# Reading M before chunk 4 in a compressed-interaction kernel: order of loads and sums at the start, and one product handed to GpSimd

## The chip, the cores and the metric

The kernel runs on one core of a Trainium2 chip. The metric is the device time of one execution in microseconds; lower is better. TensorE (PE) multiplies matrices, VectorE (DVE), ScalarE (ACT) and GpSimd (POOL) work element by element, SyncE (SP) issues most DMAs. Every engine works through its own queue in program order.

## The reference

The reference is a compressed interaction network of three layers on `x` of shape (1024, 64, 16): a batch of 1024, 64 fields, 16 embedding values.

```python
x0 = x; h = x; xs = []
for i in range(3):
    z = einsum('bfe,bge->bfge', x0, h).reshape(B, f0 * fh, E)
    y = einsum('oc,bce->boe', Ws[i], z) + bs[i][None, :, None]
    if i != 2:
        x_i, h = y[:, :64, :], y[:, 64:, :]
    else:
        x_i, h = y, y
    xs.append(x_i)
pooled = sum(concatenate(xs, axis=1), axis=2)      # (1024, 256)
return pooled @ fc_w.T + fc_b                       # (1024, 1)
```

All is float32. `W0` is (128, 64·64), `W1` and `W2` are (128, 64·64) too, since each hidden half has 64 rows.

## The kernel before, in words

Only a weighted sum of the last layer is wanted, so the kernel folds the final vector into the weights. From `W2` and `fc_w` it makes a 64 x 64 matrix (V2), and contracts the second half of `W1` with it to a 64 x 64 x 64 tensor M. What remains for every chunk of the batch are the pairwise products of the fields, x_f · x_g, contracted with two sets of 64 columns: one gives the hidden half h1, the other q, which is later multiplied with h1. M enters only through M[f,g] + M[g,f].

**Chunks and tiles.** The batch is cut into 32 chunks of 32 items (512 columns each: 32 x 16). The distinct field pairs of a chunk fill 16 tiles of 128 rows, in four groups j = 0 to 3 of four tiles each. One `product` (L248) multiplies `xa` (four shifted copies of x, 1 MB) by one quarter `xb[j]` (256 KB) into a block of 128 x 2048; 14 such blocks (`z`) are handed out in turn, first freed first used (`take`, `used`). VectorE's products read `xb[j]` from a PSUM copy (`xp`), which ScalarE makes (`second`, L566) in a bank of a two-bank rotation ("y"). GpSimd's products read `xb[j]` where it was loaded.

**The head.** Chunks 2, 3, 0, 1 come first, while weights are still made. M is computed, written to a DRAM scratch array `md`, extended to 96 x 96 rows, and read back into the block `ms` on a slant: rows (`read_rows`, two reads on each of two queues) and columns (`read_columns(j)`, one read for each half of the partitions, 64 KB each in rows of 64 floats). The diagonal goes to `va`. `q_weights(j)` (L511) adds rows and columns on VectorE into the q half of `w_all` for the tiles of group j. `last_q_weights` does that for j = 3, returns the block, and clears 32 rows of one tile. `head_q_tile` (L280) then contracts the kept products of chunks 0 and 1 with these q columns, group after group. `w_sums` makes sums and differences of weights for later (`ws`), mostly on GpSimd.

**Chunks 4 and 5** are plain: all 16 tiles are contracted with both sets of columns. Beside them run small jobs on sums of weights: `weigh` (GpSimd), `add_up` (VectorE, L553) and `place` (ScalarE, L558) make `v0`, `va` and `vb`. `x_v0x` (L303) multiplies x by V0 x, read from the banks `y`.

**Pairs.** Chunks 6 to 29 go in twelve pairs (a, b) through a scheme that saves products of matrices by working with sums and differences. For a pair, VectorE makes products X (a, j = 0, 1), B21 (a, j = 2, 3), B22 (b, j = 2, 3) and T3 (from the sum of two quarters of b, `w_both`), by `w_product` (L646). GpSimd makes six differences by `w_mix` (L661): T2 = T3 - X, T3 = B22 - T2 and T2 = T2 - B21, each for j = 0 and 1, the last two in place. TensorE (`mm`, L538) adds them into three banks, `alpha`, `beta` and `delta`. `snap_p1` and `snap_p7` (ScalarE, L669, L675) copy from alpha and delta at the middle of the pair.

**Order.** From the head's q tiles on, the program is a list of jobs with a slot number each, `at(when, fn, ...)`; the list is sorted by the number and issued in that order. So a slot is no time: it only says what stands before what in each engine's queue, and in which order blocks and banks are handed out. The pair with index n = 0 (chunks 6 and 7, k = 3) has a line of slots of its own, relative to T0 = 33; its `make_pair` takes ten slots for B22 j=2, w_both 0, T3 0, X 0, B22 j=3, w_both 1, T3 1, X 1, B21 j=2, B21 j=3, and six for the differences. The loads in lines 485 to 507 are written out by hand: their order is that of SyncE's queue.

Of the kernel before, what the change touches and what calls it, by code (L numbers as in the profile page):

```python
# [42 lines left out]
F = 64  # L43
# [25 lines left out]
def cin_kernel(ctx, tc, xra, xrb, wh, w0r, w1h, w2t, wx1, wx0, vec, out):  # L69
    nc = tc.nc  # L70
# [6 lines left out]
    halves = [slice(0, F), slice(F, 128)]  # L77

    def const_tile(name, shape):
        return const.tile(shape, F32, tag=name, name=name)  # L80
# [4 lines left out]
    def take(uses=1):  # L85
        n = vacant.pop(0)
        left[n] = uses
        return n
# [28 lines left out]
    for base in (0, 64, -64):  # L117
        nc.gpsimd.affine_select(
            out=shift, in_=shift, compare_op=ALU.not_equal, fill=1.0, base=base,
# [12 lines left out]
    va, vb, v0 = (const_tile(n, [128, F]) for n in ("va", "vb", "v0"))  # L132
# [8 lines left out]
    def load_xa(c, at=slice(0, NI)):  # L141
        if c not in xas or at.start == 0:
            xas[c] = xp.tile([128, NI, N], F32, tag="xa", name=f"xa_{c}")
        nc.sync.dma_start(
            out=xas[c][:, at, :],
            in_=bass.AP(
                tensor=xra.tensor, offset=c * XR * N + at.start * N,
                ap=[[N, 128], [1, (at.stop - at.start) * N]],
            ),
        )  # L150

    def quarter(c, j):
        xbs.setdefault(c, {})[j] = xp.tile([128, N], F32, tag="xb", name=f"xb_{c}_{j}", bufs=9)
        return xbs[c][j]

    def load_xb(c, *js):
        for j in js or range(NJ):
            nc.sync.dma_start(out=quarter(c, j), in_=xrb[c, :, j, :])
# [223 lines left out]
    for h in range(2):  # L382
        at = slice(32 * h, 32 * h + 32)
# [36 lines left out]
    row = EXT * F  # L420

    def m_ap(f1, f2, dims):
        return bass.AP(tensor=md.tensor, offset=md.offset + f1 * row + f2 * F, ap=dims)
# [3 lines left out]
    for half, queue in enumerate((nc.sync, nc.scalar)):  # L427
        queue.dma_start(
            out=m_ap(0, 32 * half, [[row, F], [1, 32 * F]]), in_=m_rows[halves[half]]
# [5 lines left out]
        out=m_ap(64, 68, [[row, 4], [4 * F, 7], [1, 4 * F]]),  # L435
        in_=m_rows[0:4, 4 * F :].rearrange("p (k c) -> p k c", c=4 * F),
# [26 lines left out]
    def skewed(f1, f2, dims):  # L463

        at = len(dims) - 2
        return m_ap(f1, f2, dims[:at] + [[row + F, F]] + dims[at:])
# [4 lines left out]
    def read_columns(j, queue, half):  # L471
        queue.dma_start(  # L472
            out=ms[halves[half], 1, j * NI : (j + 1) * NI],
            in_=skewed(0, 16 * half + 4 * (j + 1), [[row, NI], [1, F]]),
        )
# [20 lines left out]

    for half in range(2):
        read_columns(1, nc.sync, half)
    load_xa(4)
    load_xb(4, 3, 0)  # L500
    for half in range(2):
        read_columns(2, nc.sync, half)
    load_xb(4, 1)
    for half in range(2):
        read_columns(3, nc.sync, half)
    nc.sync.dma_start(out=va[halves[1]], in_=m_ap(0, 0, [[row + F, F], [1, F]]))
    load_xb(4, 2)

    def q_weights(j):
        at = slice(j * NI, (j + 1) * NI)  # L510
# [17 lines left out]
    def at(when, fn, *args, **flags):  # L528
        ops.append((when, len(ops), fn, args, flags))
# [111 lines left out]
    wh_all, wq_all = w_all[:, :, 0:64], w_all[:, :, 64:128]  # L641
    s1, s2, s3, s4, neg = (ws[:, n] for n in range(5))

    def w_product(p, c, j, name, uses):
        p.setdefault(name, {})[j % 2] = b = take(uses)
        nc.vector.tensor_tensor(  # L646
            blocks[b], xas[c], xbs[c][j].unsqueeze(1).to_broadcast([128, NI, N]), ALU.mult
        )

# [43 lines left out]
    def make_pair(t, p, when, mixed):  # L693
        a, b = p["a"], p["b"]
        for when, c, j, name, uses in (
            (when[0], b, 2, "B22", 5), (when[1], b, 0, None, 0), (when[2], b, 0, "T3", 9),
            (when[3], a, 0, "X", 5), (when[4], b, 3, "B22", 6), (when[5], b, 1, None, 0),
            (when[6], b, 1, "T3", 9), (when[7], a, 1, "X", 12 if p["k"] > 3 else 6), (when[8], a, 2, "B21", 5),
            (when[9], a, 3, "B21", 6),
        ):  # L700
            if name is None:
                at(t + when, w_both, p, j)
                continue
            if name != "T3":
                at(t + when - (3.3 if p["k"] > 4 and name == "B22" and j == 2 else 2.7), second, c, j)
            at(t + when, w_product, p, c, j, name, uses)
        for when, j, *names in zip(
            mixed, (0, 1, 0, 1, 0, 1), *zip(
                *(2 * (("T2", "T3", "X"),) + 2 * (("T3", "B22", "T2"),) + 2 * (("T2", "T2", "B21"),))
            )  # L710
        ):
            at(t + when, w_mix, p, j, *names)

    def first_fill(p):
        a = p["a"]
        return [
            (w_job, p, beta, wq_all, NI, "X"), (w_job, p, beta, wq_all, NT - NI, "B21"),
            (lambda: q_extra(a, va, p["beta"]),),
        ]

    def second_fill(p):
        return [
            (w_job, p, delta, wh_all, NI, "X"), (w_job, p, delta, wh_all, NT - NI, "B21"),
        ] + w_run(p, delta, neg, "T2")[7 - p["late"] :]

    def late_run(p):
        b = p["b"]
        return [
            (w_job, p, alpha, neg, NI, "T3"), (w_job, p, alpha, s4, NI, "B22"),
        ] + w_run(p, alpha, s4, "B22") + [(lambda: q_extra(b, vb, p["alpha"]),)]  # L730
# [8 lines left out]
    def window(t, p, fill, late, pad=[], order=GROUPS[4:] + GROUPS[:4]):  # L739
        zipped(  # L740
            t,
            w_run(p, alpha, wq_all, "X", True, order=order) + fill[0] + w_run(p, alpha, s2, "T2")
            + fill[1] + w_run(p, alpha, s1, "T3")
            + [(w_job, p, alpha, wh_all, NI, "T3"), (w_job, p, alpha, s1, NI, "B22")],
            w_run(p, delta, s3, "T3", True) + late
            + w_run(p, beta, wq_all, "B21", True, 2 * NI)
            + pad + w_run(p, delta, neg, "T2")[: 7 - p["late"]],
        )
        at(t + 30.2, squares, p)
        at(t + 6.8, snap_p1, p)  # L750
        at(t + 6.9, snap_p7, p)
        at(t + 6.8 + len(fill[0]) + 7, snap_u2, p)

    def end_pair(t, p, whens):
        hb_, qa, uub, ha, uua, xv, add = whens
        at(t + hb_, w_hb, p)
        at(t + qa, w_qa, p)
        at(t + uub, w_uu, p, alpha, "A", snaps[2])
        at(t + ha, w_ha, p)
        at(t + uua, w_uu, p, delta, "O", snaps[0])  # L760
        at(t + xv, x_v0x, p["k"])
        at(t + add, sums, p["k"])


    def load_pair(t, p, b0, a0, b1, a1):
        a, b = p["a"], p["b"]
        at(t + b0, load_xa, b)
        at(t + b0, load_xb, b, 2, 0)
        at(t + a0, load_xa, a)
        at(t + a0, load_xb, a, 0)  # L770
        at(t + b1, load_xb, b, 3, 1)
        at(t + a1, load_xb, a, 1, 2, 3)
        for c in (b, a):
            at(t + 1, load_e, c)
            at(t + 14, square, c)
        at(t + 1.1, load_xx, p["k"])
# [19 lines left out]
        at(-17, new_acc, c, tag="set")  # L796
    for m in range(NT):
        at(m - 16, head_q_tile, 0, m // NI, m % NI)
    at(-11, q_weights, 2)
    at(-7, last_q_weights)  # L800
    at(-16, w_sums, 0)
    at(-6.9, w_sums, 1)
    for j, when in enumerate((-12.3, -10.5, -6)):
# [39 lines left out]
    for n in range(NPAIR):  # L843
        k = n + 3
        s = k % 2
        p = {
            "k": k, "A": halves[s], "O": halves[1 - s], "b": 2 * k + s, "a": 2 * k + 1 - s,
            "late": 1 + n % 2 if n else 0,
        }
        pairs.append(p)  # L850
        t = T0 + SPAN * n
        if n == 0:
            load_pair(t, p, -39.9, -33.3, -33.15, -27)
            make_pair(
                t, p, (-23.4, -20.7, -20.4, -17.8, -17.2, -16.8, -16.6, -12.5, -4, 3),
                (-14, -12.4, 7.2, 12.4, 16.4, 21.7),
            )
            left5 = [[(contract_half, 5, 3, i, n) for i in (2, 3)] for n in range(2)]
            window(
                t, p, ([left5[1][0], (q_extra, 4, va)], [left5[1][1]]),  # L860
                [left5[0][0], (q_extra, 5, va), None, None], [left5[0][1], None],
                GROUPS,
            )
        else:
            q = pairs[-2]
            load_pair(t, p, -34, -28, -27.8, -27.7)
            make_pair(
                t, p, (-21.4, -18.7, -18.4, -15.8, -12.2, -9.5, -6.1, -2, 1.6, 4.2),
                (-5, 2.8, 7.2, 12.4, 16.4, 21.7),
            )  # L870
            window(t, p, (first_fill(q), second_fill(q)), late_run(q))
            end_pair(t, q, (0.7, 11.7, 17.9, 22.3, 23.2, 24, 27.5))
# [45 lines left out]
    c, k = NCH - 1, NP - 1  # L918
    t, q = T0 + SPAN * NPAIR, pairs[-1]
# [151 lines left out]
```

## Time and the profile before

| | |
|---|---|
| Time, median of 3 runs | 471.14 us (468.98 to 473.04) |
| Profiled execution | 469.04 us, span 467.2 us, mean clock 0.996 |
| TensorE busy | 457.5 us, 98% of the span |
| VectorE busy | 398.1 us, 85% |
| GpSimd busy | 329.9 us, 71% |
| ScalarE busy | 118.7 us, 25% |
| DMA | 86.04 MB, mean 184 GB/s |

A line of the profile's groups reads: line of the code, engine, operation, output<-input, times done, busy time. A wait reads "engine, line, output <- who ended it", then the total, the number and the longest. The slices divide the span into 40 parts of 11.7 us; a digit is a tenth. The span leaves out 1.8 us that the execution's own time has around it.

### The profile page before, as it was taken

To read this page: it belongs to the slowest core of one execution; us is meant where nothing else is said; L and a number is where in the kernel's file an instruction comes from. 1 tells how busy PE (TensorE), PEld (TensorE's weight loads), DVE (VectorE), ACT (ScalarE), POOL (GpSimd) and SP (SyncE) were. 2 spreads that over 40 slices of the span, in tenths; PEclk is the share of its full clock that TensorE was granted. 3 is DMA by queue.
4 is the path that set the end of the run, shared out by engine and by line. 5 is a ranking of instruction groups with operands and counts; after the bars stand their busy time and mean duration, and the time that the engine had idled before them with its cause. 6 is when DMAs were issued, how large, how long until landed. Compare 5 with 4: busy or idle time off the path is not lost.

```text
span 467.2 us, 6049 instructions
## 1 busy us (share of the span) xinstructions
PE 457.5 (98%) x2308; PEld 169.1 (36%) x2308; DVE 398.1 (85%) x283; ACT 118.7 (25%) x219; POOL 329.9 (71%) x99
## 2 busy tenths in 40 slices
PE   8999699998999999999999999999999999999997
PEld 4565143332333333333333333333333333244444
DVE  4994799599898999989898998989898998999621
ACT  3171431223323113131313213131312314222101
POOL 5333689388798979899798979899798979500000
PEclk9999899999999999999999999999999999999999
DMA  8997995193819274563818364472818555061000
GB/s 318 409 293 218 323 397 219 38 358 100 317 43 290 93 244 160 161 234 108 282 41 286 108 228 168 137 266 72 288 58 270 180 203 191 13 213 35 0 1 2
DMA packets 32609, 86.04 MB, mean 184 GB/s; under 512 B 6112, under 2 KB 6784, under 8 KB 27652
## 3 DMA queue, kind: packets, MB, share of 16 engines
q1 hardware_dynamic: 31796, 84.70, 52.7%
q10 hardware_dynamic: 784, 0.95, 0.7%
q8 instruction: 18, 0.29, 0.3%
q14 instruction: 11, 0.09, 0.1%
HBM read 84.00 MB, written 1.64 MB: 183 GB/s over the span
## 4 chain that ended last, share of the span: by engine, by line
PE 86%; DMA 8%; SPq 2%; DVE 2%; issue 1%; ACT 1%; DVEq 0%; ACTq 0%
PE alpha L538 53%; PE acc L538 16%; PE delta L538 8%; PE beta L538 7%; DMA xa<-in_xra 3%; DMA xb<-in_xrb 3%; PE acc L280 2%; DVE z L646 1%; DMA md<-z 1%; PE y L538 1%; DMA va<-md 1%; SPq L431 0%; SPq L432 0%; SPq L472 0%; DVE uu L298 0%
## 5 line engine op out<-in xcount | busy, mean ns | idle before, releaser
L661 POOL TENSOR_TENSOR z<-z,z 128x2048 f32<-128x2048 f32 x72 | 286.5, 4020 | 40.2 <-PE alpha L538 30.6
L646 DVE TENSOR_TENSOR z<-xa,xp 128x2048 f32<-128x2048 f32 x96 | 216.8, 2280 | 14.5 <-POOL z L661 12.0
L538 PE MATMUL alpha<-z,ws 128*64 128x512 f32 x576 | 196.6, 592 | 0.0
L538 PE MATMUL delta<-z,ws 128*64 128x512 f32 x336 | 150.5, 594 | 0.0
L566 ACT COPY xp<-xb 128x512 f32<-128x512 f32 x93 | 54.5, 588 | 208.0 <-DVE z L646 171.5
L538 PEld LDWEIGHTS alpha<-z,ws 128*64 128x64 f32 x576 | 61.6, 137 | 106.1 <-issue 106.0
L538 PE MATMUL beta<-z,w_all 128*64 128x512 f32 x216 | 96.9, 593 | 0.0
L538 PE MATMUL alpha<-z,w_all 128*64 128x512 f32 x192 | 86.9, 595 | 1.6 <-DVE z L646 1.4
L538 PE MATMUL acc<-z,w_all 128*64 128x512 f32 (+3 forms) x320 | 77.2, 509 | 0.0
L248 DVE TENSOR_TENSOR z<-xa,xp 128x2048 f32<-128x2048 f32 (+2 forms) x33 | 67.6, 2087 | 7.5 <-DMA va<-md 5.3
L538 PEld LDWEIGHTS delta<-z,ws 128*64 128x64 f32 x336 | 44.7, 137 | 9.2 <-issue 9.2
L538 PEld LDWEIGHTS alpha<-z,w_all 128*64 128x64 f32 x192 | 25.4, 137 | 59.5 <-issue 48.2
L538 PEld LDWEIGHTS acc<-z,w_all 128*64 128x64 f32 (+1 forms) x320 | 32.2, 148 | 35.8 <-issue 35.7
L538 PEld LDWEIGHTS beta<-z,w_all 128*64 128x64 f32 x216 | 29.0, 137 | 13.9 <-issue 13.9
L262 PE MATMUL acc<-z,w_all 128*64 128x256 f32 x256 | 29.1, 382 | 0.8 <-DVE z L248 0.7
L248 POOL TENSOR_TENSOR z<-xa,xb 128x2048 f32<-128x2048 f32 x4 | 18.2, 4554 | 15.5 <-DMA xb<-in_xrb 15.4
L262 PEld LDWEIGHTS acc<-z,w_all 128*64 128x64 f32 x256 | 18.0, 137 | 13.0 <-DVE z L248 2.3
L538 PE MATMUL delta<-z,w_all 128*64 128x512 f32 x48 | 22.6, 592 | 0.0
L298 DVE SCALAR_TENSOR_TENSOR uu<-acc,vs,snap 64x512 f32<-64x512 f32 (+2 forms) x5 | 3.2, 644 | 20.1 <-ACT snap L291 20.1
L307 DVE TENSOR_REDUCE acc<-uu 128x64 f32<-128x1024 f32 (+3 forms) x20 | 20.2, 1016 | 0.2
L280 PE MATMUL acc<-z,w_all 128*64 128x512 f32 x64 | 15.8, 652 | 4.0 <-DVE w_all L511 4.0
L652 DVE TENSOR_TENSOR xp<-xp,xb 128x512 f32<-128x512 f32 x24 | 16.8, 699 | 0.8
(101 smaller groups left out, 299.9 us busy)
## 6 DMA issues: line engine op xcount, KB each, us to landing
xa<-in_xra SPq DMA_DIRECT2D x32, 1024.0 KB, 4.7
xb<-in_xrb SPq DMA_DIRECT2D x128, 256.0 KB, 6.7
e<-in_xra SPq DMA_DIRECT2D x28, 128.0 KB, 4.1
xx<-in_xra SPq DMA_DIRECT2D x28, 128.0 KB, 2.5
z<-in_w2t SPq DMA_DIRECT2D x2, 1024.0 KB
z<-in_wx SPq DMA_DIRECT2D x2, 1024.0 KB, 9.0
z<-in_w1h SPq DMA_DIRECT2D x1, 1024.0 KB
xa<-in_xra SPq DMA_DIRECT2D x3, 256.0 KB
```

The lines of the kernel that those rows point to most:

```text
L248: engine.tensor_tensor(blocks[zs[c, j]][:, at, :], xas[c][:, at, :], xbs[c][j].unsqueeze(1).to_broadcast([128, last - first, N]), ALU.mult,)
L262: nc.tensor.matmul(accs[c][halves[n]], w_all[:, t, 0:64], blocks[zs[c, j]][:, i, n * H2 : (n + 1) * H2], start=(t == 0), stop=(j == last a ...
L280: nc.tensor.matmul(accs[c][halves[1 - c % 2]], w_all[:, t, 64:128], blocks[zs[c, j]][:, i, :], start=(t == 0), stop=False, skip_group_chec ...
L298: nc.vector.scalar_tensor_tensor(uu[h, 0, cols], acc_c[h], bh1[h], q, ALU.add, ALU.mult)
L307: nc.vector.tensor_reduce(acc[rows, of, k, half], uu[rows, of if at is None else at, E * half.start : E * half.stop].rearrange("p k (b e) ...
L538: nc.tensor.matmul(out, w, rhs, start=start, stop=stop, skip_group_check=True)
L566: nc.scalar.copy(bank, xbs[c][j])
L646: nc.vector.tensor_tensor(blocks[b], xas[c], xbs[c][j].unsqueeze(1).to_broadcast([128, NI, N]), ALU.mult)
L652: nc.vector.tensor_tensor(bank, bank, xbs[p["b"]][j], ALU.add)
L661: nc.gpsimd.tensor_tensor(blocks[o][:, tiles], blocks[x][:, tiles], blocks[y][:, tiles], ALU.subtract)
```

## The change

Three edits. In the loads written out by hand, the column reads for j = 2 and 3 and the read of M's diagonal into `va` go ahead of the load of chunk 4's `xa` and of its four quarters, which were threaded between them before; in the job list, `q_weights(2)` and `last_q_weights` get slots ahead of all three of VectorE's products of chunk 4. In pair 0, B21 j=2 is made by GpSimd, straight from the loaded quarter and without ScalarE's copy, and its slot stands between GpSimd's first two differences. X 1, "the last operand", and the difference that uses it get later slots, just ahead of `x_v0x` (slot 28.5).

```diff
     for half in range(2):
         read_columns(1, nc.sync, half)
+    for j in (2, 3):
+        for half in range(2):
+            read_columns(j, nc.sync, half)
+    nc.sync.dma_start(out=va[halves[1]], in_=m_ap(0, 0, [[row + F, F], [1, F]]))
     load_xa(4)
-    load_xb(4, 3, 0)
-    for half in range(2):
-        read_columns(2, nc.sync, half)
-    load_xb(4, 1)
-    for half in range(2):
-        read_columns(3, nc.sync, half)
-    nc.sync.dma_start(out=va[halves[1]], in_=m_ap(0, 0, [[row + F, F], [1, F]]))
-    load_xb(4, 2)
+    load_xb(4, 3, 0, 1, 2)
...
-    def w_product(p, c, j, name, uses):
+    def w_product(p, c, j, name, uses, engine=nc.vector):
         p.setdefault(name, {})[j % 2] = b = take(uses)
-        nc.vector.tensor_tensor(
+        engine.tensor_tensor(
...
             if name is None:
                 at(t + when, w_both, p, j)
+                continue
+            if name == "B21" and j == 2 and p["k"] == 3:
+                at(t + when, w_product, p, c, j, name, uses, engine=nc.gpsimd)
                 continue
...
-    at(-11, q_weights, 2)
-    at(-7, last_q_weights)
+    at(-15, q_weights, 2)
+    at(-14, last_q_weights)
...
             make_pair(
-                t, p, (-23.4, -20.7, -20.4, -17.8, -17.2, -16.8, -16.6, -12.5, -4, 3),
-                (-14, -12.4, 7.2, 12.4, 16.4, 21.7),
+                t, p, (-23.4, -20.7, -20.4, -17.8, -17.2, -16.8, -16.6, -7, -13.5, 3),
+                (-14, -6.9, 7.2, 12.4, 16.4, 21.7),
             )
```

## The prediction

> **What bounds the kernel now.** Five views, from coarse to fine. First the page's slices: TensorE is at nine tenths or more in nearly every slice, so a microsecond counts only if TensorE waits in it. The third line is the clock granted to it.
>
> ```profile
> PE   8999699998999999999999999999999999999997
> ...
> PEclk9999899999999999999999999999999999999999
> ```
>
> The one low busy digit past the start is slice 5 (46.7 to 58.4 us), and the only low clock digit is the same slice. Second, the waits of TensorE (total us, times, longest):
>
> ```profile
> PE acc L280 <- DVE w_all L511: 4.0, 1, 4.0
> PE alpha L538 <- DVE z L646: 1.4, 1, 1.4
> ```
>
> All other waits of TensorE are under 1 us. The first is the head's q tiles (L280) waiting for a sum of M (L511), the second is the start of pair 1's window. Third, busy time by windows in that slice (after the span: PE, PEld, DVE, ACT, POOL, then clock, DMA share, GB/s):
>
> ```profile
> 50.00:52.00 2.00, 0.00 (x0) 0.00 (x0) 2.00 (x1) 0.59 (x1) 2.00 (x1) 1.00 1.05 292
> 52.00:54.00 2.00, 0.79 (x4) 0.40 (x6) 2.00 (x3) 0.88 (x2) 0.87 (x1) 0.93 0.88 342
> 54.00:56.00 2.00, 2.00 (x6) 0.48 (x4) 1.90 (x4) 1.99 (x4) 0.00 (x0) 0.50 0.96 355
> 56.00:58.00 2.00, 2.00 (x10) 0.60 (x8) 2.00 (x1) 0.78 (x3) 1.83 (x3) 0.72 1.05 410
> ```
>
> TensorE stands still, then runs at half clock. Fourth, the chain that ended last, through the same place (start, us, what):
>
> ```profile
> 40.23 7.15 DMA xa<-in_xra
> 47.38 0.02 issue
> 47.39 2.49 DMA va<-md
> ...
> 52.09 1.08 DVE w_all L511
> 53.16 0.04 issue
> 53.21 8.78 PE acc L280 x32
> ```
>
> The sum is not waiting for M alone: it stands behind chunk 4's load. Fifth, the timelines of VectorE and GpSimd:
>
> ```profile
> 49.88 2.29 DVE L248 TENSOR_TENSOR z<-xa,xp 128x2048 f32<-128x2048 f32 x1 [5.33 <-DMA va<-md]
> 52.09 1.07 DVE L511 TENSOR_TENSOR w_all<-z 128x256 f32<-128x256 f32 x1
> ...
> 48.36 4.51 POOL L248 TENSOR_TENSOR z<-xa,xb 128x2048 f32<-128x2048 f32 x1 [1.17 <-DMA xb<-in_xrb]
> ```
>
> VectorE idles 5.33 us in front of chunk 4's first product; q_weights(2) is queued behind that product. The releaser printed is va, but the product reads no va: ScalarE's copy of xb(4,0), which ended at 49.79, released it.
>
> [...] 4.0 us of idling, then 0.50 and 0.72, and 32 matmuls that took 7.04 us before the gap take 8.78 after it. [...] L511 takes 0.41 to 0.43 us three times and 1.07 once, beside GpSimd's product; products with xp in PSUM keep 2.28 us beside GpSimd. [...] M's columns are rows of 256 B: with 663 packets under 512 B, the window 48 to 50 moved 203 GB/s at 0.86 DMA share, against 398 GB/s in 58 to 60.
>
> **Part 1: the M reads and their sums go first.** Removed is the wait of 4.0 us, and with it the slow clock: 8.78 - 7.04 = 1.74. Ceiling **5.74 us**. Is M in time? SyncE issues the four column reads in 1.56 + 1.37 us right after columns 1, from 40.2 to 43.1. Columns 1 were issued by 40.12 and their sum ran at 44.12, 4.0 later; the same gives about 47.1 for all of M. At the pace of the sums 0 and 1 (40.39 to 44.12, 3.7 a step) it is 47.8 and 51.5. TensorE needs j=2 at 49.23 and j=3 3.5 us later, at 52.75, so either pace is enough. GpSimd's w_sums(0) (two of 1.27 us, from 44.69) may hold a sum up as above, by at most 1.3 us. Cost: nothing.
>
> Price: xa(4) is issued behind 1.56 + 1.37 + 0.47 = 3.4 us of SyncE's time, at 43.6 instead of 40.23, and xb(4,...) behind it. Data of xa(4) began to flow at 42.0, 1.8 after its issue, so now at 45.4. Ahead of product (4,0) come xa(4), xb(4,3) and xb(4,0): 1.57 MB. At the 296 GB/s of 42 to 48 that is 5.3 us: 50.7, and 0.3 for the end, 51.0. At the 7.2 us of before (42.0 to 49.2, small reads among it) it is 52.6. ScalarE's copy takes 0.6, so VectorE starts (4,0) at s = 51.6 to 53.2, against 49.88. I take **s = 51.9**.
>
> TensorE ends the head at 56.3 and wants chunk 4 at 56.8; the first product is ready at s + 2.3 = 54.2, and each next 2.2 later for 3.4 of TensorE's time. GpSimd's (4,3) moves to some 51 to 55.5, wanted at 67. No stall. VectorE now runs five products back to back (11.1 us) without the two sums, the memset and the waits among them: 63.0, where it was at 63.58. Chunks 5 to 7 follow in the old order, and the small reads that slowed 46 to 52 are gone from there, so I leave their landing as it is.
>
> **Part 2: pair 0.** From B22,2 to the end of the second add_up VectorE works for 80.9 - 63.58 = 17.3 us without a wait: it ends at s + 28.4 = 80.3. The next items are the ones the new slots reorder. Before:
>
> ```profile
> 80.82 2.28 DVE L646 TENSOR_TENSOR z<-xa,xp 128x2048 f32<-128x2048 f32 x1
> 87.89 1.61 DVE L303 SCALAR_TENSOR_TENSOR uu<-y,cx,xx 128x512 f32<-128x512 f32 x2 [4.79 <-PE y L538]
> 89.42 1.27 DVE L307 TENSOR_REDUCE acc<-uu 128x32 f32<-128x512 f32 x2
> ```
>
> The first is X,1. Its ScalarE copy stood ahead of the placing of va and vb; its new slot puts it behind these (4 x 0.24 us). So X,1 starts at s + 28.4 + 0.95 + 0.65 = s + 30.0, and the two V0 x products, queued behind it, end 2.3 + 1.6 later, at s + 33.9. alpha and delta of pair 0 take the PSUM banks of y 0 and y 2 (four banks in rotation), so TensorE cannot begin the pair before. With the full gain it would begin at 91.25 - 5.74 = 85.5; s + 33.9 is 85.8. A new stall of **0.3 us**; from the ends of s, 0 to 1.6.
>
> GpSimd's B21,2 costs 4.51 us (its product row[...]). It follows T2,0, which ends at 82.0, so it runs 82.0 to 86.5, then T2,1 (3.44) to 90.0. B21,2 is wanted at 94.4, T2,1 at 97.0. T3 in place then starts at 90.0 where TensorE's release alone would give 95.04 - 5.4 = 89.6; T2 in place ends at 102.4, where TensorE wants it at 107.79 - 5.4 = 102.4. Nothing, with no slack left. By the order of the block list, B21,2 gets chunk 4's j=2 block, which TensorE leaves at about 67: no wait. VectorE is rid of 2.28 us and ScalarE of one copy of 0.59, but pair 1's first product waits for a ScalarE copy queued behind the snaps of pair 0's alpha and delta, so it moves with TensorE. The chain from it to pair 1's X,1 (99.17 to 116.40, VectorE without a wait) is untouched: the 1.4 us stall stays. Gain there: nothing.
>
> **Sum.** 4.0 + 1.74 - 0.3 = 5.4 us. From pair 1 on, nothing changes. The profiled execution took 469.04 (span 467.2, 1.8 around it), so 463.6; it is at the low end of the runs shown (median 471.14, which would give 465.7). I forecast **464.4**.
>
> **The rivals.** (a) The V0 x products cost more. If alpha waits for the sums after them too (the trace names L307 as releaser of alpha's weight load, though that load keeps its 0.43 us cadence), the stall grows by 1.3; with s = 52.5 it is 0.9 + 1.3, and the gain 3.5: 465.5. (b) Relief of VectorE also takes away the wait at pair 1: 5.4 + 1.4 = 6.8, 462.2. The copy behind the snaps speaks against it. (c) Slower: chunk 4's operands stand behind the small reads. Its place is VectorE's queue; it decides from s = 57.3 on, when s + 33.9 passes 91.25. If the reads go at 3.7 us a step, M is in at 51.5, operands follow after 7.2 us, s = 59.3, pair 0 starts at 93.2 instead of 91.25: 471.0, and each microsecond more is one more. For it: the sums 0 and 1 were 3.7 apart. Against: 500 small packets, the size of two column reads, moved within 40 to 42, and columns 1 shared their time with the row reads. (d) The change does not do what it says, TensorE waiting at L280 as before: the sums cannot stand behind a product once they are ahead of it, so I give it nothing apart.
>
> **How the numbers follow.** Forecast 0.58, (a) 0.20, (b) 0.08, (c) 0.14. Over the spread of runs, the forecast alone is 461.5 to 467; the bounds of s and (a), (b), (c) widen that to 460 to 470.5. The measurement tells about 1% (4.7 us) from no change. Of the forecast 0.49 lies beyond 1% faster, with (b) 0.57; the rest of it, (a) and some of (c) are within, 0.35; (c) at s over 62 is slower, 0.08.
>
> **What would show it.** L280 as 64 matmuls in one run of some 14.1 us ending at about 56.3, a clock of 1.00 from 50 to 60, L511's last two at 46 to 49 us and ahead of L248's first on xa(4). Product (4,0) at 51.9 tells s. A gap of some 0.3 us ahead of pair 0's alpha; GpSimd's extra product at 82 to 86.5; the 1.4 us wait for pair 1's X,1 still there. Wrong if TensorE waits for z of chunk 4, if a new wait over 1.5 us stands ahead of alpha, or if chunk 4's operands land after 53.

## The result and the profile after

The changed kernel takes 463.51 us (median of 4 runs, 463.28 to 464.88) against 470.74 us before on the same chip (median of 4, one run more than in the table of the kernel before): a ratio of 0.985, 95% interval 0.9802 to 0.9897. It is faster, by 7.2 us between the medians; forecast was 464.4. Its profiled execution took 463.37 us with a span of 461.6, so between the two profiled executions the gain is 5.7 us (5.6 by the spans). Why the medians show 1.5 us more is settled below.

The slices of the page after, busy and granted clock of TensorE:

```profile
PE   8999999999999999999999999999999999999997
...
PEclk9999999999999999999999999999999999999999
```

Slice 5 has lost its low digits. The waits of TensorE after (total us, times, longest):

```profile
PE acc L262 <- DVE z L248: 1.1, 1, 1.1
PE misc L113 <- PEq L1060: 0.8, 1, 0.8
PE alpha L535 <- DVE z L643: 0.5, 1, 0.5
```

The wait at L280 is not there; what is left is the program's start (L262) and the wait for pair 1's X,1, now 0.5 us. The windows of the place where TensorE stood:

```profile
50.00:52.00 2.00, 2.00 (x12) 0.68 (x10) 0.14 (x1) 0.59 (x1) 1.42 (x1) 1.00 1.05 394
52.00:54.00 2.00, 2.00 (x12) 0.61 (x10) 2.00 (x1) 0.59 (x1) 2.00 (x1) 1.00 1.03 422
54.00:56.00 2.00, 2.00 (x12) 0.57 (x8) 2.00 (x2) 1.78 (x4) 2.00 (x2) 1.00 0.99 370
```

TensorE is full there, and at full clock. The timelines of TensorE, SyncE's queue and VectorE after:

```profile
42.45 13.90 PE L280 MATMUL acc<-z,w_all 128*64 128x512 f32 x64
...
44.30 0.52 SPq L144 DMA_DIRECT2D xa<-in_xra  x1
...
44.40 2.27 DVE L508 TENSOR_TENSOR w_all<-z 128x256 f32<-128x256 f32 x2 [0.85 <-DMA z<-md]
...
51.86 11.08 DVE L248 TENSOR_TENSOR z<-xa,xp 128x2048 f32<-128x2048 f32 x5 [5.01 <-ACT xp L563]
...
82.10 2.29 DVE L643 TENSOR_TENSOR z<-xa,xp 128x2048 f32<-128x2048 f32 x1 [1.64 <-ACT xp L563]
84.30 1.40 DVE L303 SCALAR_TENSOR_TENSOR uu<-y,cx,xx 128x512 f32<-128x512 f32 x2
85.62 1.27 DVE L307 TENSOR_REDUCE acc<-uu 128x32 f32<-128x512 f32 x2
...
85.61 0.59 PE L535 MATMUL alpha<-z,w_all 128*64 128x512 f32 x1
85.76 0.64 PE L535 MATMUL delta<-z,ws 128*64 128x512 f32 x1
```

L280 is one run of 64 records (each matmul stands in the trace as two). M's last two sums (L508 now) end at 46.7, 2.7 us before TensorE is half through L280 (42.45 + 13.90 / 2 = 49.4) and wants them. VectorE idles about as long as before, 5.0 us against 5.3, but with no sum queued behind that TensorE needs. Then five products run back to back.

### The profile page after: what moved, and what is told of

The parts are those of the page before. It is cut to its first block, busy times and chain, and to the rows that moved or that the text cites. A ratio compares the mean times of both kernels' runs of the same rounds, so it can differ in the third digit from the quotient of the medians.

```text
span 461.6 us, 6055 instructions
## 1 busy us (share of the span) xinstructions
PE 456.3 (99%) x2308; PEld 171.9 (37%) x2308; DVE 396.5 (86%) x282; ACT 118.1 (26%) x218; POOL 334.7 (73%) x100
## 3 DMA queue, kind: packets, MB, share of 16 engines
q1 hardware_dynamic: 31796, 84.70, 53.7%
HBM read 84.00 MB, written 1.64 MB: 186 GB/s over the span
## 4 chain that ended last, share of the span: by engine, by line
PE 94%; DVE 2%; DMA 2%; issue 1%; SPq 0%; ACT 0%; DVEq 0%; ACTq 0%
PE alpha L535 53%; PE acc L535 16%; PE delta L535 8%; PE beta L535 7%; PE acc L262 6%; PE acc L280 3%; DMA z<-in_w0r 2%; DVE z L643 1%; PE y L535 1%; PE pm L399 0%; PE pv L372 0%; DVE uu L298 0%; SPq L144 0%; PE xp L219 0%; DVE xp L649 0%
## 5 line engine op out<-in xcount | busy, mean ns | idle before, releaser
L643 DVE TENSOR_TENSOR z<-xa,xp 128x2048 f32<-128x2048 f32 x95 | 214.5, 2280 | 15.5 <-POOL z L658 12.0
L535 PE MATMUL alpha<-z,w_all 128*64 128x512 f32 x192 | 86.9, 595 | 0.7 <-DVE z L643 0.5
L535 PEld LDWEIGHTS acc<-z,w_all 128*64 128x64 f32 (+1 forms) x320 | 32.5, 147 | 35.6 <-issue 33.9
L262 PE MATMUL acc<-z,w_all 128*64 128x256 f32 x256 | 29.1, 382 | 1.3 <-DVE z L248 1.1
L262 PEld LDWEIGHTS acc<-z,w_all 128*64 128x64 f32 x256 | 18.0, 137 | 13.6 <-DVE z L248 2.8
L307 DVE TENSOR_REDUCE acc<-uu 128x64 f32<-128x1024 f32 (+3 forms) x20 | 20.2, 1016 | 0.2
L179 ACT ACTIVATE e<-e 64x512 f32<-64x512 f32 x28 | 16.1, 622 | 4.1 <-DMA e<-in_xra 4.0
```

The costliest lines, as they stand in the source:

```text
L179: nc.scalar.activation(es[c][halves[1]], es[c][halves[0]], AF.Square)
L262: nc.tensor.matmul(accs[c][halves[n]], w_all[:, t, 0:64], blocks[zs[c, j]][:, i, n * H2 : (n + 1) * H2], start=(t == 0), stop=(j == last a ...
L307: nc.vector.tensor_reduce(acc[rows, of, k, half], uu[rows, of if at is None else at, E * half.start : E * half.stop].rearrange("p k (b e) ...
L535: nc.tensor.matmul(out, w, rhs, start=start, stop=stop, skip_group_check=True)
L643: engine.tensor_tensor(blocks[b], xas[c], xbs[c][j].unsqueeze(1).to_broadcast([128, NI, N]), ALU.mult)
```

## Experiments

The start of the program differs from one execution to the next: L280 begins anywhere from 42.2 to 45.0 us. TensorE waits up to 2.5 us for the first products in the head, and in the two latest starts (part 1 alone and B21,2 on VectorE, 44.97 and 44.71) it then runs at half clock for 3.4 us (the mean clock of both executions is 0.996). So I compare spans also **from L280's first matmul on**. Each row is one profiled execution; "gap" is the wait for the sum, "second half" the last 32 records of L280. The ratio to the kernel before comes from timed runs.

| kernel | L280 begins | gap | second half | from L280 to the end | ratio (95%) |
|---|---|---|---|---|---|
| before, first profile | 42.19 | 3.98 | 8.78 | 425.0 | |
| before, second | 42.32 | 4.92 | 9.83 | 427.1 | |
| before, third | 43.02 | 4.75 | 9.97 | 427.0 | |
| after, first profile | 42.45 | none | 13.90 for both halves | 419.2 | 0.985 (0.9802 to 0.9897) |
| after, second | 42.92 | none | 13.90 for both | 419.2 | |
| part 1 alone | 44.97 | none | 13.90 for both | 419.3 | 0.9864 (0.9818 to 0.991) |
| part 2 alone | 43.54 | 5.09 | 9.74 | 427.2 | 1.0005 (0.9981 to 1.0028) |
| loads alone | 42.67 | 6.76 | 8.98 | 428.0 | 1.0033 (1.0021 to 1.0045) |
| sums alone | 42.61 | 4.63 | 9.96 | 426.9 | 0.9986 (0.9959 to 1.0013) |
| gap filled | 43.22 | 0.78 | 7.09 | 423.6 | 0.9922 (0.9893 to 0.995) |
| copy early | 43.18 | none | 13.90 for both | 419.4 | 0.9842 (0.9817 to 0.9867) |
| B21,2 on VectorE | 44.71 | none | 13.90 for both | 421.4 | 0.9895 (0.9868 to 0.9922) |
| more reads | 43.21 | none | 13.90 for both | 425.6 | 0.9958 (0.9934 to 0.9982) |

My theory: the gap at L280 and the slow clock after it are the whole gain. The main rival: the relief of VectorE in pair 0 carries part of it.

**Part 1 alone.** The changed kernel with pair 0's old slots and B21,2 back on VectorE:

```diff
-            if name == "B21" and j == 2 and p["k"] == 3:
+            if False:
...
-                t, p, (-23.4, -20.7, -20.4, -17.8, -17.2, -16.8, -16.6, -7, -13.5, 3),
-                (-14, -6.9, 7.2, 12.4, 16.4, 21.7),
+                t, p, (-23.4, -20.7, -20.4, -17.8, -17.2, -16.8, -16.6, -12.5, -4, 3),
+                (-14, -12.4, 7.2, 12.4, 16.4, 21.7),
```

> Only the moved reads and the moved sums; pair 0 as in the kernel before. Theory A (the wait of TensorE for the sum of M and the slow clock after it are the whole gain): span within 0.4 us of the changed kernel's 461.6, time within 0.3% of it; pair 0's alpha begins at about 85.5, VectorE begins pair 1 at about 93.5, and TensorE waits some 1.4 us for pair 1's X,1. Theory B (the relief of VectorE in pair 0 by 2.28 us carries part of the gain): about 464, pair 1 begins 2 us later.

The raw span, 464.3, misses the 0.4 us of theory A, but by its start: L280 began 2.5 us later than in the changed kernel's profile. From there on it takes 419.3 us, against 419.2, and the timed median is 464.84, 0.29% above 463.51 (the ratios, each taken on one chip, are 0.9864 and 0.985). alpha of pair 0 begins 43.2 us after L280 does (88.14 - 44.97), as after (85.61 - 42.45 = 43.2), and the wait for X,1 is there as forecast:

```profile
113.46 0.64 PE L535 MATMUL alpha<-z,w_all 128*64 128x512 f32 x1 [1.57 <-DVE z L643]
```

So part 1 alone has the gain that can be measured.

**Part 2 alone.** The changed kernel with the reads and the sums' slots of before.

```diff
-    at(-15, q_weights, 2)
-    at(-14, last_q_weights)
+    at(-11, q_weights, 2)
+    at(-7, last_q_weights)
```

(and lines 497 to 507 as before)

> Only pair 0's new slots and GpSimd's B21,2; reads and sums as in the kernel before. Theory A: span 467 to 467.5 as before, L280 still waits 4.0 us, the clock still falls, and pair 1's first product stays at about 99.2 since ScalarE's copy behind the snaps holds it. Theory B: 1.4 to 2.3 us faster than before, span 465 to 466.

Twelve runs give 1.0005. The profile's span is 470.7, longer than either theory said, but the same gap and the same slow clock stand in it (5.09 and 9.74 us), and X,1 is waited for by 1.44 us as before. VectorE's first product of pair 1 waits for ScalarE's copy:

```profile
102.59 2.29 DVE L646 TENSOR_TENSOR z<-xa,xp 128x2048 f32<-128x2048 f32 x1 [2.67 <-ACT xp L566]
```

Part 2 by itself is worth nothing: theory B falls.

**Loads alone, sums alone.** The kernel before with only the reads moved, and the kernel before with only the two sums' slots changed.

> Only the moved reads; the sums keep their slots behind chunk 4's products, pair 0 as before. Theory A: M is in by 47, but q_weights(2) stands behind product (4,0), which starts at about 51.9, and may be held by GpSimd's product until about 55.2; TensorE waits 5 to 6.3 us at L280 and the clock falls, the head ends at 63 to 64.5 instead of 62: 470 to 471.5 against the profiled 469.0. Theory C (the late landing of M is the cause, not its place in VectorE's queue): a gain of 3 us or more.

> Only the moved sums; the reads stay threaded between chunk 4's loads, pair 0 as before. If M's columns land before GpSimd's product (4,3) starts at 48.4, or if a sum can run beside that product, TensorE waits under 1 us and the gain is 4 to 5.5 us: 463.5 to 465. If the columns land later and the product then holds the sum [...], q_weights(2) ends at about 53.3 as before, TensorE waits 4 us, product (4,0) slips to about 53.8, and the gain is 0: about 469.

With the loads alone M's reads have all been issued by 44.6, 1.0 us later than in the changed kernel, whose sums use them from 44.4 on; yet the sum stands in VectorE's queue behind product (4,0), which itself starts later:

```profile
52.89 2.29 DVE L248 TENSOR_TENSOR z<-xa,xp 128x2048 f32<-128x2048 f32 x1 [8.51 <-ACT xp L563]
55.09 1.32 DVE L508 TENSOR_TENSOR w_all<-z 128x256 f32<-128x256 f32 x1
```

The gap grows to 6.76 us, the ratio is 1.0033. Theory C falls: the early landing is worth nothing here to a sum that stands behind a product. With the sums alone, the second branch came true in the profiled execution. VectorE and GpSimd in that kernel:

```profile
50.77 3.45 DVE L511 TENSOR_TENSOR w_all<-z 128x256 f32<-128x256 f32 x1 [6.16 <-DMA z<-md]
...
49.44 4.50 POOL L248 TENSOR_TENSOR z<-xa,xb 128x2048 f32<-128x2048 f32 x1 [2.19 <-DMA xb<-in_xrb]
```

M's columns land at 50.7, behind chunk 4's operands, and by then GpSimd's product has begun: the sum, which took 0.41 to 0.43 us in this kernel's other three, takes 3.45 us and ends 0.3 us after that product (54.22 against 53.94). With the loads alone, where GpSimd's product ran from 51.61 for 4.51 us, the sum took 1.32 us and also ended 0.3 us after it, and so it was in the first profile of the kernel before, with 1.07 us. So, as a rule, both moves are needed, and the reads' place also decides whether the sum meets GpSimd's product. One of the twelve timed runs took 466.93 us at a mean clock of 1.00: there the sums alone seem to have been in time, as in the first branch, but no trace of that run shows it.

**The gap filled.** The kernel before, with eight matmuls of zero weights (16 records) ahead of group 2, so that TensorE works through the gap. Each `warm` issues two matmuls with zeros as weights, which add zero to the sums of chunks 0 and 1; its definition is left out here:

```diff
+    for m in range(4):
+        at(-8.5 + 0.01 * m, warm)
     at(-11, q_weights, 2)
```

> The kernel before with eight more matmuls of zero weights (some 3.5 us) ahead of the head's q tiles of group 2, adding zero to the sums there: TensorE is kept at work in the gap, which stays. Theory A: L280's second half takes 7.0 us instead of 8.8, the clock stays at 1.00, the sum still arrives at about 53.2: 1.7 us faster than before, span about 465.5. Rival (the slow stretch comes of the loads or the data, not of idling): span as before, 467.2.

TensorE's timeline there:

```profile
50.09 3.60 PE L288 MATMUL acc<-z,const-float32-0.0 128*64 128x512 f32 x16
54.47 7.09 PE L280 MATMUL acc<-z,w_all 128*64 128x512 f32 x32 [0.78 <-DVE w_all L518]
```

The sum comes no earlier, but the second half takes 7.09 us at full clock: 1.00 in each window of 2 us from 50 to 66. So the slow stretch comes of idling: after the 0.78 us left of it here the clock stayed at 1.00, after 3.98 us in the kernel before it fell to 0.50. The gain is larger than the 1.7 us of theory A: 471.74 to 468.49, 3.2 us. The two repeated executions of the kernel before, shown below, lose 2.8 and 2.9 us to the slow clock.

**Copy early.** The changed kernel, with the ScalarE copy for pair 1's first product ahead of pair 0's snaps:

```diff
-                at(t + when - (3.3 if p["k"] > 4 and name == "B22" and j == 2 else 2.7), second, c, j)
+                at(t + when - (3.3 if p["k"] > 3 and name == "B22" and j == 2 else 2.7), second, c, j)
```

> The changed kernel, with ScalarE's copy for pair 1's first product put ahead of the snaps of pair 0's alpha and delta. Theory A (that copy holds VectorE's start of pair 1, and the chain from there ends in TensorE's wait for X,1): pair 1's first product starts at about 92.7 instead of 93.5, the wait of 0.5 us for X,1 goes, span 461.1. Rival (GpSimd's differences hold pair 0, so another wait takes its place): 461.6.

```profile
91.87 4.49 DVE L643 TENSOR_TENSOR z<-xa,xp 128x2048 f32<-128x2048 f32 x2
...
101.93 2.29 DVE L643 TENSOR_TENSOR z<-xa,xp 128x2048 f32<-128x2048 f32 x1 [0.32 <-issue]
```

VectorE's first product of pair 1 now follows pair 0's last without the 0.82 us of idling before it. But its fourth then waits 0.32 us, right after a ScalarE copy that stands behind another snap, and TensorE still waits 0.45 us for X,1. The time is that of the changed kernel. Another wait took the place, though not the one on GpSimd that the rival named: GpSimd's difference does make delta's step in pair 0 late here too, by 1.0 us, but what TensorE still waits for when that step is done is X,1. In this execution s was 1.0 us later than in the changed kernel's, so the sizes are not to be compared closer.

**B21,2 at its new slot, on VectorE.** `if False:` in place of the condition that hands it to GpSimd, slots as changed.

> The changed kernel, with B21,2 at its new slot but made by VectorE, with ScalarE's copy as before. Theory A: at that slot it stands between the two add_ups, va and vb come 2.3 us later, X,1 and the V0 x products with them, and alpha of pair 0 begins at about 88.0 instead of 85.6: span about 463.9. Rival (the gap ahead of alpha has slack, or is made up later): 461.6 to 462.

```profile
78.70 2.28 DVE L550 TENSOR_REDUCE shift<-z 128x32 f32<-128x2048 f32 x1
80.90 2.28 DVE L643 TENSOR_TENSOR z<-xa,xp 128x2048 f32<-128x2048 f32 x1
83.09 2.28 DVE L550 TENSOR_REDUCE shift<-z 128x32 f32<-128x2048 f32 x1
...
90.01 1.07 PE L535 MATMUL alpha<-z,w_all 128*64 128x512 f32 x2 [1.29 <-DVE uu L303]
```

The product stands between the two add_ups. alpha begins 45.3 us after L280 does, 2.1 later than after (43.2), and from L280 to the end it takes 2.2 us more. The chain add_up, va and vb, copy, X,1, V0 x sets pair 0's start, and it has no slack.

**More reads.** The changed kernel with eight further column reads ahead of chunk 4's load:

```diff
+    for n in range(8):
+        nc.sync.dma_start(
+            out=snaps[n // 2][halves[n % 2], 0 : NI * F],
+            in_=skewed(0, 16 * (n % 2) + 12, [[row, NI], [1, F]]),
+        )
     load_xa(4)
```

> The changed kernel with eight more column reads of M (64 KB each, into tiles that are not yet used) between va and chunk 4's load. Theory A (chunk 4's operands stand behind what SyncE issues first, 0.7 us each, and pair 0's alpha begins at s + 33.9, s being the start of product (4,0)): s is about 57.5 instead of 51.9, TensorE waits some 3 us for chunk 4's first block and the clock falls, alpha begins at about 91.4, span 467 to 468, no gain left. Rival (reads and loads overlap on the 16 DMA engines): s under 54, gain of 3 us or more left.

SyncE's queue, and what VectorE and TensorE then waited for:

```profile
45.54 5.21 SPq L504 DMA_DIRECT2D snap<-md  x8
50.86 0.54 SPq L144 DMA_DIRECT2D xa<-in_xra  x1
...
59.35 8.88 DVE L248 TENSOR_TENSOR z<-xa,xp 128x2048 f32<-128x2048 f32 x4 [11.37 <-ACT xp L568]
...
61.69 26.07 PE L540 MATMUL acc<-z,w_all 128*128 128x512 f32 x80 [4.04 <-DVE z L248]
92.74 1.07 PE L540 MATMUL alpha<-z,w_all 128*64 128x512 f32 x2 [0.37 <-DVE uu L303]
```

Eight reads take 5.21 us of SyncE's time. From L280, s comes at 16.1 us instead of 9.4, 6.7 later; alpha at 49.5 instead of 43.2, 6.4 later. TensorE idles 4.0 us for chunk 4 and runs slow after it (80 matmuls in 26.07 us, 24.43 before). The span is 468.8, and 0.4% of gain is left by the timed runs, where theory A said 467 to 468 and none. From L280 on it loses 1.4 us less than the repeated executions of the kernel before (425.6 against 427.0): after its gap the clock is at half for 3.4 us, after theirs for 6.8 us (shown below). The overlap that the rival hoped for is not there.

**Before and after again.** Unchanged copies, for the 1.5 us between medians and profiles.

> The kernel before once more, unchanged, for the difference of its median (471) from its first profiled execution (469.0). Theory A: the wait at L280 and the slow clock after it cost more in most executions than the 4.0 + 1.74 us of that one: wait 4.5 to 5.5 us, L280's second half 9 to 10 us. Theory B: only the start of the program, before L280, varies: wait 4.0, second half 8.8, L280 begins after 43.

> As the run before it: the same two theories, a second execution.

> The changed kernel once more, unchanged. Theory A: from L280's start to the end it takes within 0.5 us of the 419.2 us of its first profile, whenever L280 begins, since nothing waits there. Theory B: the same, so this run only tells how far L280's start moves (42.5 in the first).

```profile
54.27 9.83 PE L280 MATMUL acc<-z,w_all 128*64 128x512 f32 x32 [4.92 <-DVE w_all L511]
...
54.80 9.97 PE L280 MATMUL acc<-z,w_all 128*64 128x512 f32 x32 [4.75 <-DVE w_all L511]
```

Theory A holds: in both repeated executions of the kernel before (471.14 and 471.81 us) the gap and the second half cost more than in its first profile, 4.92 + 2.79 and 4.75 + 2.93 over the 7.04 us of a half at full clock, against 3.98 + 1.74. The windows of the first repeated execution show where the second term comes from (columns as before; the clock is the third from the end):

```profile
52.00:54.00 2.00, 0.00 (x0) 0.00 (x0) 2.00 (x2) 0.89 (x2) 1.94 (x1) 0.75 1.02 410
54.00:56.00 2.00, 1.73 (x4) 0.53 (x6) 2.00 (x2) 1.99 (x4) 0.00 (x0) 0.50 0.90 301
56.00:58.00 2.00, 2.00 (x8) 0.71 (x6) 1.90 (x4) 0.85 (x3) 0.92 (x1) 0.50 1.09 418
58.00:60.00 2.00, 2.00 (x6) 0.48 (x4) 2.00 (x2) 0.69 (x2) 1.84 (x3) 0.54 0.99 414
```

A window of 2 us with a clock of 0.50 is 2 us at half clock, one with 0.75 is 1 us. So the clock was at half for 1.0 + 2.0 + 2.0 + 1.8 = 6.8 us; the windows of the first profile, shown in the prediction, give 0.3 + 2.0 + 1.1 = 3.4 us. The mean clock tells the same of executions without a trace: 3.4 us at half clock lower the mean of a span of 469 us by 3.4 x 0.5 / 469 = 0.0036. Of the 39 runs of the kernel before that stand beside the first four experiments, 12 show 0.996, one such stretch by this count, and took 469.9 us on average; 23 show 0.992 or 0.993, two stretches, and took 471.5; 4 show 0.989, three by this count, and took 472.9 (no trace shows where their third lies). All four runs of the changed kernel show 1.00, and it takes 419.2 us from L280 in both of its traces. So the first profile of before was an execution in which the place was cheap, and 427.0 - 419.2 = 7.8 us is what the repeated ones lose there. The start adds its own spread: part 1 alone, which has no gap, ran from 463.68 to 466.07.

## Why the prediction was right

**The wait and the clock.** The mechanism was right: the gap goes, the clock stays at 1.00 from 40 to 70 us, the head ends at 56.28 where 56.3 was forecast. For the execution that it was read from, the sum was right too: 469.04 - 5.4 = 463.6, and the changed kernel's profile took 463.37. That the clock falls for the idling could be no more than an estimate from one trace, 3.98 us of idling and then 0.50; the filled gap shows it. Two things were off. The step "4.0 + 1.74" was called the ceiling, but it is the loss of one cheap execution, with 3.4 us at half clock; the repeated ones, with 6.8 us, lose 7.7. And the forecast was laid 0.8 above the sum for the spread of the runs, though that spread belonged in good part to the place that the change removes; the time came out 0.9 below the forecast. The gain of the medians is 7.2, not 5.4.

**M in time.** The sums ended at 46.7; 47.1 was taken. The two beside GpSimd's w_sums took 2.27 us together instead of 0.85, inside the allowance of 1.3 us for each.

**s.** Taken as 51.9 from bounds of 51.6 to 53.2; it was 51.86. That is luck in part, since two misses cancel: xa(4) was issued at 44.30, not 43.6, and from there to s it took 7.6 us, not 8.3. Counted from L280's start, s comes at 9.4 and 9.7 us in the two executions of the changed kernel and at 10.4 with the copy early; 9.7 was forecast.

**The V0 x products.** They end at 85.70, where s + 33.9 gave 85.8. alpha began at 85.61 and delta at 85.76: a stall of 0.15 us where 0.3 was forecast. The sums after them (L307) run from 85.62 to 86.9, so rival (a)'s gate is refuted: alpha does not wait for them, and the trace's naming of L307 before was a coincidence of times.

**GpSimd.** "Nothing, with no slack left" was wrong by 0.9 us in place and right in the end. weigh's second run waited 0.44 us for its load, and the difference T2 ended at 103.0 instead of the 102.4 forecast. GpSimd and TensorE after:

```profile
98.45 4.55 POOL L658 TENSOR_TENSOR z<-z,z 128x2048 f32<-128x2048 f32 x1
...
101.72 0.59 PE L535 MATMUL acc<-z,w_all 128*64 128x512 f32 x1
102.11 1.45 PE L535 MATMUL alpha<-z,ws 128*64 128x512 f32 x3
103.05 0.64 PE L535 MATMUL delta<-z,ws 128*64 128x512 f32 x1
```

delta's step starts at 103.05, as soon as the difference is done, 0.9 us after its turn (before, it came 107.79 - 91.25 = 16.54 us after alpha; 85.61 + 16.54 = 102.15); matmuls of alpha that stood behind it are late with it. No wait shows this, since TensorE is still busy by the model of its ends. It cost nothing: the wait for pair 1's X,1 shrank from 1.44 to 0.51, by the same 0.9. Pair 1 began at 110.80 instead of 116.44, 5.64 earlier, and the spans differ by 5.6. In the second execution of the changed kernel delta's step was 1.4 us late and the wait for X,1 was gone; from alpha to pair 1 it took 25.3 us, against 25.2 in the first and before.

**The rivals.** (b) fell: relief of VectorE alone did not make TensorE begin pair 1 earlier, as the copy behind the snaps held VectorE (part 2 alone). (c) is real as a mechanism, and the formula s + 33.9 held when s was pushed 6.7 us up, but the reads did not queue as slowly as it needed: s stayed 5.4 us short of its point. (d) had been given nothing, rightly.

## What to carry to other kernels

Look at what stands ahead, in its engine's queue, of the instruction that the bound engine waits for (with the loads alone the sum came at 55.09, behind a product that began at 52.89): here neither the earlier data nor the earlier slot helped alone, save perhaps in one run of twelve; both together did. Price such a wait with the slow clock that follows it, here 1.7 to 2.9 us, and from several executions, since this wait on transfers differed from run to run (3.98, 4.92 and 4.75 us). The mean clock of each timed run tells, without a trace, how long it ran slow: 0.996 went with 3.4 us at half clock here, 0.993 with 6.8. When a second engine is relieved, ask what starts its next piece of work: here a copy on a third engine did, so 2.3 us of relief were worth nothing.

## What the runs showed of the hardware that I had not expected

The cost of the slow clock did not grow with the idle time ahead of it: 4.0 us of idling lost 1.74, 6.8 us lost 1.94, 4.6 us lost 2.92. After a single gap the clock was at half for either 3.4 or 6.8 us, and what was lost is half of the part of that stretch in which TensorE has work. Read from windows of 0.1 us:

| kernel | idle from | work again | half clock from | to | half of the work in it | lost |
|---|---|---|---|---|---|---|
| before, first profile | 49.2 | 53.2 | 53.7 | 57.1 | 1.7 | 1.74 |
| more reads (chunk 4) | 57.6 | 61.7 | 61.6 | 65.0 | 1.6 | 1.64 |
| sums alone | 49.7 | 54.3 | 53.3 | 60.1 | 2.9 | 2.92 |
| before, third | 50.1 | 54.8 | 53.8 | 60.6 | 2.9 | 2.93 |
| before, second | 49.4 | 54.3 | 53.0 | 59.8 | 2.8 | 2.79 |
| part 2 alone | 50.6 | 55.7 | 54.2 | 61.1 | 2.7 | 2.70 |
| loads alone | 49.7 | 56.5 | 53.5 | 60.3 | 1.9 | 1.94 |

Where TensorE was back at work before the clock fell, or within 0.1 us of it, the stretch was 3.4 us; where it came back 1.0 us or more after, the stretch was twice as long. That is what these seven show; they do not show why. The clock fell 3.6 to 4.5 us after the idling began. A shorter gap did it too: in the head, waits of 2.5 us (part 1 alone) and 2.4 us (B21,2 on VectorE) were followed by 3.4 us at half clock; waits of 1.5 us (part 2 alone and copy early) were not.

A 0.43 us sum on VectorE that met a GpSimd product 1.3 us into its run of 4.50 us was held for the whole rest of it, 3.45 us in all (sums alone); no run here shows why.
